# Gram stages whose first transfers go out between TensorE's first chunks, a 3x3 convolution that begins slot by slot, and smaller first loads, in a two-layer bottleneck kernel

## The chip, the core and the metric

The kernel runs on one core of a Trainium2 chip. The time is device microseconds of one execution, from three executions of the same program. A profile of one more execution gives the times of the single instructions. TensorE multiplies matrices, VectorE (DVE), ScalarE (ACT) and GpSimd (POOL) work on elements, and SyncE (SP), ScalarE and GpSimd issue DMA transfers. Everything is float32.

## What is computed

Two bottleneck layers follow one another on a batch of 64 images with 1024 channels of 14 x 14 pixels. Each layer is a 1x1 convolution to 256 channels, a 3x3 convolution and a 1x1 convolution back to 1024, each followed by a batch normalization over the whole batch, with a residual at the end:

```python
def _bn(x, gamma, beta):
    mean = jnp.mean(x, axis=(0, 2, 3), keepdims=True)
    var = jnp.var(x, axis=(0, 2, 3), keepdims=True)
    xn = (x - mean) * jax.lax.rsqrt(var + EPS)
    return gamma.reshape(1, -1, 1, 1) * xn + beta.reshape(1, -1, 1, 1)
out = jax.nn.relu(_bn(_conv(x, w1, b1, 1, 0), g1, be1))
out = jax.nn.relu(_bn(_conv(out, w2, b2, 1, 1), g2, be2))
out = _bn(_conv(out, w3, b3, 1, 0), g3, be3)
out = jax.nn.softplus(residual_scale)[0] * out
out = x + out
return jax.nn.relu(out)
```

A batch normalization needs the statistics of all pixels before the first pixel can go on. That cuts each layer into stages, and at each cut TensorE waits until the statistics are there.

## The kernel before

The 256 middle channels lie as two **slots** of 128 partitions each in one resident tile `y` of 128 x 2 x 12544 elements (12544 pixels, the whole batch). The stages, with their place in the profile in microseconds:

- **First 1x1 convolution** (0 to 308). `plain_conv1` does images 0 and 1 of the pixel tiles, with weights `w` that `load_w1` brings in four transfers on ScalarE's queue and pixel tiles `x` that `load_x` brings on SyncE's queue (the first tile in four transfers). All later tiles go through `Conv1`, a product scheme with seven multiplications in place of eight (class `Seven`), whose weight sums `ws` `combine_w1` makes on VectorE. Beside it the 3x3 filters of both layers are transformed (`filters`) and written to memory as `u`.
- **3x3 convolution** (308 to 599), `conv2`. It works on groups of 8 images (eight groups), each as six products over rows (L657 `Products`), in three pairs. For the first group `first_norm` normalizes the pixels (ScalarE the rows from 7 on, VectorE rows 0 to 6), slot 1 first; `combine` makes the row combinations `t`, `r`, the half sums `sums`, the differences `diffs` and `v`, and fetches the filters `ua` and `ub` for each product. TensorE multiplies into `even`, `odd`, `m` and `l`, and `finish` puts the results together on VectorE. The scales and shifts of the normalization come from `affine_by_slot` (L1119), which calls `affine` once for each slot before `conv2` begins.
- **Gram stage** (600 to 687), `gram`. The statistics of the third convolution are not taken from its results. They follow from the sum and the Gram matrix (256 x 256) of the normalized pixels, which needs all pixels transposed. The stage goes in 49 **chunks** of 256 pixels. For the first six (`FIRST`) and the last one (`LAST`) TensorE transposes against an identity (`by_tensor`, L942, then a VectorE copy, L948, into one of six buffers `zt`). For the other 42 VectorE transposes blocks of 32 x 32 (`by_vector`, L954), from a copy in which blocks of 32 partitions have been laid out side by side. `spread(k)` makes that copy for six chunks by 16 transfers of 96 KB from `y` into one of two homes (`ws` and `home`): ten on SyncE's queue, six on GpSimd's. Before any of that, every piece of `y` is normalized on ScalarE (L538, in `bounds`) and has a constant subtracted on VectorE (`less`, L1248). Each chunk ends in four Gram products on TensorE (`cp`, `ap`).
- **End of the statistics, third convolution and residual** (687 to 1300 for layer 0, with the first convolution of layer 1 woven in; 1677 to 2002 for layer 1).

Layer 1 repeats the 3x3 convolution from 1300 and the Gram stage from 1592.

What sets the order of work around the change: each engine runs its instructions in the order in which they stand. A planner may move an instruction ahead of its place in the program, unless it was recorded with `keep_in_program_order`; TensorE's instructions and the VectorE transposes (L954) have that, the `less` pieces, the copies into `zt` and the small operations of `affine` do not. All `norm` and `less` pieces stand in the program ahead of the first `spread`, and both `spread(0)` and `spread(1)` stand ahead of the first chunk:

```python
bounds = [0, CH * P, 3 * CH * P, *range(GPX, NPX + 1, GPX)]
for a, e in zip(bounds, bounds[1:]):
    for s in range(MS):
        y = y_all[:, s, a:e]
        norm(s, y, aff)
        less(s, y)
...
ready = [spread(k) for k in range(2)]
```

With `start = FIRST * CH * P`, the first `spread` covers pixels 1536 to 3071, for which the pieces up to pixel 3136 must be ready.

Of the kernel before, what the change touches and what calls it, by code (L numbers as in the profile page):

```python
# [41 lines left out]
P = 128  # L42
# [14 lines left out]
FIRST, LAST = 6, 1  # L57
# [36 lines left out]
def bottlenecks(ctx: ExitStack, tc: tile.TileContext, x, w1s, w2s, w3s, pars, out):  # L94
# [40 lines left out]
    def load_w1(pool, b, queue):  # L135

        w = pool.tile([P, MS, 2, CS // 2, P], FP, tag="w1", name=f"w1_{b}")
        for h in range(2):
            for o in range(MS):
                queue.dma_start(out=w[:, o, h], in_=w1s[b][:, o, h])  # L140
        return w
# [398 lines left out]
    def norm_vector(s, y, aff):  # L540
        scale, shift = aff
        nc.vector.tensor_scalar(y, y, scale[:, s : s + 1], shift[:, s : s + 1], ALU.mult, ALU.add)
        nc.vector.tensor_scalar(y, y, 0.0, None, ALU.max)

    def conv2(psum, pool, b, par, aff, stats):
# [29 lines left out]
        def stt(to, a, by, c):  # L575
            nc.vector.scalar_tensor_tensor(to, a, by, c, ALU.mult, ALU.add)  # L576

        def combine(g, pair, before=None):
# [4 lines left out]
            def ready(i, r):  # L583
                lines = (full if i in (3, 4) else RT) * GI
                r = r.rearrange("p s r (i w) -> p s (r i) w", i=GI)

                def half(tag):
                    return pool.tile([P, MS, RT * GI, WH], FP, tag=tag, name=tag, bufs=BUFS[tag])[:, :, :lines]

                sums, diffs = half("sums"), None  # L590
                nc.vector.tensor_add(sums, r[:, :, :, WH:], r[:, :, :, :WH])  # L591
                if i in FOUR:
                    diffs = half("diffs")
                    nc.gpsimd.tensor_sub(diffs, r[:, :, :, :WH], r[:, :, :, WH:])  # L594
                    v = pool.tile([P, MS * RT * GI * W], FP, tag="v", name="v", bufs=BUFS["v"])
                    v = v[:, : MS * lines * W].rearrange("p (s l c) -> p s l c", s=MS, c=W)
                    q = r.rearrange("p s l (q c) -> p (s l) q c", q=2)
                    nc.vector.tensor_sub(
                        v[:, :, :, 1 : W - 1].rearrange("p s l (q c) -> p (s l) q c", q=2),
                        q[:, :, :, 1:], q[:, :, :, : WH - 1],  # L600
                    )
                    nc.scalar.activation(v[:, :, :, 0], r[:, :, :, 0], AF.Copy)
                    nc.scalar.activation(v[:, :, :, W - 1], r[:, :, :, W - 1], AF.Copy, scale=-1.0)
                    r = v

                u = []
                for tag, a, e in (("ua", 0, 1), ("ub", 1, NKS[i])):
                    n = MS * MS * (NK - 1 if a else 1) * P
                    v = pool.tile([P, n], FP, tag=tag, name=tag, bufs=BUFS[tag])
                    v = v[:, : MS * MS * (e - a) * P].rearrange("p (s o k m) -> p s o k m", s=MS, o=MS, m=P)  # L610
                    nc.sync.dma_start(
                        out=v.rearrange("p s o k m -> p (s o) (k m)"),
                        in_=us[b][i][:, :, :, a:e].rearrange("p s o k m -> p (s o) (k m)"),
                    )
                    u.append(v)
                return Products(i, lines, r, sums, diffs, u, first=g == 0 and i == order[0][0])

            both = slice(0, MS)
            if pair[0] == 1:
                t1, t2 = new("t"), new("t")  # L620
                slots = [both] if before is None else [slice(s, s + 1) for s in reversed(range(MS))]
                for part in slots:
                    if before is not None:
                        before(part.start)
                    last(t1, g, 2, -3.0, part)
                    last(t2, g, 1, -3.0, part)
                    for s in range(part.start, part.stop):
                        stt(t1[:, s, :full], rows(g, s, 2, 0, full), -4.0, rows(g, s, 4, 0, full))
                        stt(t2[:, s, :full], rows(g, s, 1, 0, full), -4.0, rows(g, s, 3, 0, full))
                    nc.vector.tensor_add(ra[:, part], t1[:, part], t2[:, part])  # L630
# [227 lines left out]
        def first_norm(s):  # L858

            top = 7  # L860
            norm(s, y_grp[:, s, 0, top:], aff)
            norm_vector(s, y_grp[:, s, 0, :top], aff)
# [47 lines left out]
    def gram(psum, pool, homes, aff, less, beside):  # L910
# [7 lines left out]
        zts = itertools.cycle(zts)  # L918
        start = FIRST * CH * P

        bounds = [0, CH * P, 3 * CH * P, *range(GPX, NPX + 1, GPX)]
        for a, e in zip(bounds, bounds[1:]):
            for s in range(MS):
                y = y_all[:, s, a:e]
                norm(s, y, aff)
                less(s, y)

        def spread(k):

            x = homes[k % 2][:, : MS * STEP].rearrange("p (s j f) -> p s j f", s=MS, j=4)  # L930
            for i, j in itertools.product(range(4), range(4)):
                queue = nc.gpsimd if (4 * i + j) % 8 in (2, 5, 7) else nc.sync
                a = start + k * STEP + i * RUN
                queue.dma_start(out=x[32 * i : 32 * i + 32, :, j], in_=y_all[32 * j : 32 * j + 32, :, a : a + RUN])
            return x.rearrange("p s j f -> p (s j) f")

        def by_tensor(a):
# [10 lines left out]
            nc.vector.tensor_copy(zt[:, :, :M], tp.rearrange("p (c m) -> p c m", c=CH))  # L948
# [12 lines left out]
        def pairs():  # L961
            for i in range(FIRST):
                yield by_tensor(i * CH * P)
            for k in range(STEPS):
                x = ready.pop(0)
                for i in range(RUN // (CH * 32)):
                    yield by_vector(x, i)
                if k + 2 < STEPS:
                    ready.append(spread(k + 2))
            for i in range(LAST):  # L970
                yield by_tensor(NPX - (LAST - i) * CH * P)

        ready = [spread(k) for k in range(2)]
# [138 lines left out]
    def aggregate(stats, first):  # L1112
        n = stats.shape[1]
        mv = small.tile([P, n, nc.vector.BN_AGGR_DIM], FP, tag=f"mv{n}", name="mv")
        for o in range(n):
            nc.vector.bn_aggr(mv[:, o, :], stats[:, o, first:, :].rearrange("p t f -> p (t f)"))
        return mv

    def affine_by_slot(stats, first, par, g, be, order):  # L1119

        both = [small.tile([P, MS], FP, tag=f"by_slot_{n}", name=n) for n in ("scale", "shift")]
        for s in order:
            mv = aggregate(stats[:, s : s + 1], first)
            affine(mv, 1, par, g + s, be + s, to=[v[:, s : s + 1] for v in both])
        return both

    def affine(mv, n, par, g, be, conv_bias=None, to=None):

# [3 lines left out]
        v, sd, r, q = tl("v"), tl("sd"), tl("r"), tl("q")  # L1134
        nc.scalar.activation(sd, mv[:, :, 1], AF.Sqrt, bias=eps)
        nc.vector.tensor_scalar(v, mv[:, :, 1], EPS, None, ALU.add)
        nc.vector.reciprocal(r, sd)

        scale, shift = to or (tl("scale"), tl("shift"))
        nc.vector.tensor_mul(q, r, v)  # L1140
        nc.vector.scalar_tensor_tensor(q, q, -0.5, r, ALU.mult, ALU.mult)
        nc.vector.tensor_mul(r, r, par[:, g : g + n])
        nc.vector.scalar_tensor_tensor(scale, q, 1.5, r, ALU.add, ALU.mult)
        if conv_bias is None:
            off = mv[:, :, 0]
        else:
# [3 lines left out]
            nc.vector.tensor_add(off, mv[:, :, 0], bias)  # L1150
            nc.vector.tensor_sub(off, off, bias)
        nc.vector.scalar_tensor_tensor(shift, off, -1.0, scale, ALU.mult, ALU.mult)
        nc.vector.tensor_add(shift, shift, par[:, be : be + n])
        return scale, shift

    def softplus(par):
# [6 lines left out]
        u, w, l, d, z = tl("u"), tl("w"), tl("l"), tl("d"), tl("z")  # L1163
# [24 lines left out]
    with tc.tile_pool(name="first", bufs=1) as one, tc.tile_pool(  # L1188
# [4 lines left out]
        pair = [load_x(xpool, 0, t, 4 if t == 0 else 2) for t in range(2)]  # L1193
        for b in range(2):
            p = keep.tile([P, NPAR], FP, tag=f"par{b}", name=f"par{b}")
            nc.scalar.dma_start(out=p, in_=pars[b][:, :NPAR])
            par.append(p)
        masks.make_identity(nc, ident)
# [24 lines left out]
    for b in range(2):  # L1223
        pb = par[b]
        sp = softplus(pb)
        minus_c = keep.tile([P, MS], FP, tag="minus_c", name="minus_c")
        nc.vector.tensor_scalar(minus_c, pb[:, BE2 : BE2 + MS], 0.0, -1.0, ALU.max, ALU.mult)

        aff = affine_by_slot(stats1, T - 3 + b, pb, G1, BE1, (1, 0))
        stats2 = keep.tile([P, MS, 1 + len(LAST_PARTS), nc.vector.BN_STATS_DIM], FP, tag="stats2", name=f"stats2_{b}")  # L1230
        with tc.tile_pool(name=f"conv2_{b}", bufs=1) as pool, ExitStack() as scope:
            conv2(Psum(scope, ["l"], l=2, m=2, odd=2, even=2), pool, b, pb, aff, stats2)

        with tc.tile_pool(name=f"last_{b}", bufs=1) as one, tc.tile_pool(
# [5 lines left out]
            aff = affine(aggregate(stats2, 0), MS, pb, G2, BE2)  # L1240
            with ExitStack() as scope:
# [4 lines left out]
                with tc.tile_pool(name=f"gram_{b}", bufs=1) as pool:  # L1246
                    def less(k, y):
                        nc.vector.tensor_scalar(y, y, minus_c[:, k : k + 1], None, ALU.add)  # L1248

# [15 lines left out]
                    grams = gram(psum, pool, homes, aff, less, beside)  # L1265
# [6 lines left out]
                aff = affine(mv3, CS, pb, G3, BE3, conv_bias=B3)  # L1272
                for a in aff:
                    nc.vector.tensor_scalar(a, a, sp, None, ALU.mult)
# [48 lines left out]
```

## Time and profile before

| what | before |
| --- | --- |
| median of three executions | 2007.07 us (2005.67 to 2010.76) |
| the profiled execution | 2004.56 us, span 2002.8 us |
| TensorE (PE) busy | 1945.9 us, 97% of the span |
| VectorE (DVE) busy | 1586.3 us, 79% |
| ScalarE (ACT) busy | 948.3 us, 47% |
| GpSimd (POOL) busy | 618.5 us, 31% |
| chain that ended last | PE 79%, DVE 13%, DMA 4% |
| first convolution, TensorE's first matmul | at 5.89 us |
| 3x3 convolution, first matmul on data | at 315.85 us (layer 0), 1308.10 us (layer 1) |
| Gram stage, first transpose on TensorE | at 604.59 us (layer 0), 1595.90 us (layer 1) |
| memory traffic | 267.95 MB read, 115.87 MB written |

The span is the time between the first and the last instruction of the profiled execution; its device time is 1.8 us longer. "Busy" is the time in which an engine worked on an instruction. The chain that ended last goes back from the last instruction, at each step to what released it. TensorE is busy for all but 57 us of the span, so what can be won without less arithmetic lies in those microseconds, and in stretches in which TensorE's granted clock is low: the profile gives that clock as a share of full speed for each stretch.

### The profile page before, as it was taken

The numbers are of one execution on the slowest core, as the hardware profiler recorded it, in microseconds if no ns is written. First come the engines' busy times: TensorE is split into PE (matmuls) and PEld (weight loads), VectorE is DVE, ScalarE is ACT, GpSimd is POOL, SyncE is SP. The second block draws the span as 40 slices with busy tenths as digits, with TensorE's granted clock in tenths as the row PEclk, the third lists the DMA queues.
The fourth block names the chain that finished last, engine by engine and source line by source line (L and its number), as shares of the span: only waits on it lengthen the run. The fifth ranks groups of instructions, "written<-read, shape, count | busy, mean of one in ns | idle before, by whom it ended". The sixth has DMA issues, their size and how long they took to land.

```text
span 2002.8 us, 27581 instructions
## 1 busy us (share of the span) xinstructions
PE 1945.9 (97%) x9560; PEld 1640.7 (82%) x9560; DVE 1586.3 (79%) x2842; ACT 948.3 (47%) x1933; POOL 618.5 (31%) x690
## 2 busy tenths in 40 slices
PE   8999998999997999999999999999999889999999
PEld 4555557999996889999999999989999877555554
DVE  5788758999986567776776777699999865899997
ACT  1322214366655055555555555444656631555555
POOL 0111101122214123334333333212121140666665
PEclk9999999999997999999999999999999999999999
DMA  7866724555546624444444444265656375699998
GB/s 270 285 251 248 256 97 164 179 190 197 181 142 177 215 105 185 162 185 170 167 188 161 176 179 163 96 204 176 199 178 199 117 183 199 252 335 331 340 339 298
DMA packets 176219, 407.65 MB, mean 204 GB/s; under 512 B 12368, under 2 KB 143504, under 8 KB 159568
## 3 DMA queue, kind: packets, MB, share of 16 engines
q1 hardware_dynamic: 162208, 330.44, 48.4%
q10 hardware_dynamic: 5328, 50.86, 6.1%
q0 software_dynamic: 8544, 24.59, 3.7%
q8 instruction: 76, 1.25, 0.2%
q14 instruction: 63, 0.52, 0.1%
HBM read 267.95 MB, written 115.87 MB: 192 GB/s over the span
## 4 chain that ended last, share of the span: by engine, by line
PE 79%; DVE 13%; DMA 4%; ACT 1%; issue 1%; POOL 1%; SPq 1%; DVEq 0%; ACTq 0%
PE ay L171 16%; PE cy L171 13%; PE cp L171 11%; PE ap L171 10%; PE odd L171 5%; PE even L171 5%; PE ax L171 5%; PE m L171 5%; PE l L171 4%; PE cx L171 4%; DMA x<-mid 2%; DVE x L455 2%; DVE sums L591 1%; PE ps L171 1%; DMA out<-x 1%
## 5 line engine op out<-in xcount | busy, mean ns | idle before, releaser
L329 ACT ACTIVATE cu<-cy,scale 128x196 f32<-128x196 f32 (+1 forms) x552 | 257.4, 475 | 295.9 <-PE cy L171 288.3
L329 ACT ACTIVATE x<-x,shift 128x392 f32<-128x392 f32 x368 | 211.8, 614 | 68.8 <-POOL x L481 52.9
L455 DVE SCALAR_TENSOR_TENSOR x<-cp,scale,x 128x196 f32<-128x196 f32 (+1 forms) x368 | 178.0, 484 | 82.5 <-PE cp L171 81.1
L594 POOL TENSOR_TENSOR diffs<-r 128x448 f32<-128x448 f32 (+1 forms) x80 | 111.5, 1405 | 424.5 <-DVE r L576 263.4
L171 PE MATMUL cy<-ct,ws 128*128 128x196 f32 (+1 forms) x736 | 222.0, 383 | 2.5 <-ACT cu L329 2.5
L476 POOL TENSOR_TENSOR x<-x,cu 128x196 f32<-128x196 f32 (+1 forms) x184 | 167.4, 910 | 170.8 <-ACT cu L329 170.7
L171 PE MATMUL ay<-at,ws 128*128 128x196 f32 (+1 forms) x752 | 209.4, 382 | 1.0 <-ACT au L329 1.0
L481 POOL TENSOR_TENSOR x<-x,cu 128x392 f32<-128x392 f32 x124 | 125.8, 1014 | 191.1 <-DVE x L455 186.4
L171 PEld LDWEIGHTS ay<-at,ws 128*128 128x128 f32 x752 | 136.4, 190 | 35.0 <-ACT au L329 2.0
L171 PEld LDWEIGHTS cy<-ct,ws 128*128 128x128 f32 x736 | 133.7, 190 | 36.9 <-ACT cu L329 3.8
L502 POOL TENSOR_TENSOR x<-x,cu 128x392 f32<-128x392 f32 x120 | 125.0, 1042 | 82.7 <-DVE x L455 77.6
L171 PE MATMUL m<-sums,ua 128*128 128x224 f32 (+1 forms) x752 | 145.5, 336 | 0.0
L171 PE MATMUL cp<-zt 128*128 128x257 f32 x392 | 123.0, 396 | 16.2 <-DVE zt L954 16.2
L171 PEld LDWEIGHTS m<-sums,ua 128*128 128x128 f32 x752 | 131.4, 190 | 0.2
L455 DVE SCALAR_TENSOR_TENSOR x<-cx,scale,x 128x196 f32<-128x196 f32 (+1 forms) x184 | 89.2, 485 | 50.5 <-PE cx L171 50.1
L171 PE MATMUL cy<-y,w 128*128 128x196 f32 (+1 forms) x404 | 126.0, 398 | 0.0
L171 PE MATMUL cx<-y,w 128*128 128x196 f32 (+1 forms) x404 | 125.2, 396 | 0.0
L171 PE MATMUL even<-v,ub 128*128 128x224 f32 (+1 forms) x640 | 123.8, 335 | 0.7 <-ACT even L688 0.7
L171 PE MATMUL odd<-v,ub 128*128 128x224 f32 (+1 forms) x640 | 123.9, 335 | 0.2
L171 PE MATMUL l<-diffs,ub 128*128 128x224 f32 (+1 forms) x640 | 122.0, 334 | 0.0
L329 ACT ACTIVATE au<-ay 128x196 f32<-128x196 f32 (+1 forms) x141 | 53.8, 381 | 139.7 <-PE ay L171 139.0
L171 PE MATMUL cp<-y,ws 128*128 128x196 f32 (+1 forms) x368 | 113.9, 391 | 2.5 <-DVE x L455 1.0
(215 smaller groups left out, 4355.9 us busy)
## 6 DMA issues: line engine op xcount, KB each, us to landing
x<-in_x SPq DMA_DIRECT2D x62, 1568.0 KB, 6.8
ub<-u SPq DMA_DIRECT2D x80, 768.0 KB, 4.8
x<-mid SPq DMA_DIRECT2D x32, 1568.0 KB, 10.1
mid<-x ACTq DMA_DIRECT2D x31, 1568.0 KB, 5.2
out<-x SPq DMA_DIRECT2D x124, 392.0 KB, 6.7
ua<-u SPq DMA_DIRECT2D x96, 256.0 KB, 3.1
ub<-u SPq DMA_DIRECT2D x16, 1024.0 KB, 6.2
u<-y POOLq DMA_DIRECT2D x40, 256.0 KB, 6.3
```

The costliest lines, as they stand in the source:

```text
L171: tc.keep_in_program_order(nc.tensor.matmul(*args, **kw))
L329: tc.keep_in_program_order(nc.scalar.activation(*args, **kw))
L455: nc.vector.scalar_tensor_tensor(v, bank, self.scale[:, o : o + 1], v, ALU.mult, ALU.add)
L476: nc.gpsimd.tensor_add(self.part(1, 1), self.part(1, 1), u3)
L481: nc.gpsimd.tensor_add(v, v, self.u12)
L502: nc.gpsimd.tensor_add(v, v, self.u12[:, i * self.n : (i + 1) * self.n])
L591: nc.vector.tensor_add(sums, r[:, :, :, WH:], r[:, :, :, :WH])
L594: nc.gpsimd.tensor_sub(diffs, r[:, :, :, :WH], r[:, :, :, WH:])
```

## The change

Five edits, in the order of the kernel's stages.

**Smaller first loads.** The first of the four weight transfers is cut in two, and the first pixel tile comes in eight transfers in place of four. The softplus of both layers' residual scale is computed at the start of the program, where before each layer asked for its own at the start of its second stage.

```diff
+        n = CS // 2
+        for h, o in itertools.product(range(2), range(MS)):
+
+            step = n // 2 if b == h == o == 0 else n
+            for s in range(0, n, step):
+                queue.dma_start(out=w[:, o, h, s : s + step], in_=w1s[b][:, o, h, s : s + step])
...
-        pair = [load_x(xpool, 0, t, 4 if t == 0 else 2) for t in range(2)]
+        pair = [load_x(xpool, 0, t, CS if t == 0 else 2) for t in range(2)]
...
+        sps = [softplus(p) for p in par]
```

**The 3x3 convolution begins slot by slot.** `affine_by_slot` is gone. `first_norm(s)` now computes the scale and shift of its own slot first, so the order on VectorE is: statistics, scale and normalization of slot 1, its `t` and `r`, and then the same for slot 0. VectorE takes rows 0 to 5 in place of 0 to 6. These VectorE operations are recorded in program order. The filters of the very first product come as four transfers: `ub` for slot 1, `ub` for slot 0, then `ua` for each; before, they were `ua` and then `ub`, one transfer each.

```diff
         def first_norm(s):
 
-            top = 7
+            affine_of(s)
+            top = 6
             norm(s, y_grp[:, s, 0, top:], aff)
             norm_vector(s, y_grp[:, s, 0, :top], aff)
...
+                first = g == 0 and i == order[0][0]
+                u = {}
+                for tag, a, e in (("ub", 1, NKS[i]), ("ua", 0, 1)) if first else (("ua", 0, 1), ("ub", 1, NKS[i])):
...
+                    for part in [slice(1, 2), slice(0, 1)] if first else [slice(0, MS)]:
+                        nc.sync.dma_start(
+                            out=v[:, part].rearrange("p s o k m -> p (s o) (k m)"),
+                            in_=us[b][i][:, part, :, a:e].rearrange("p s o k m -> p (s o) (k m)"),
+                        )
```

**The small operations of `affine`** stand in program order; the negated mean is made early, and for up to two slots the shift is one operation per slot in place of two operations in a row:

```diff
+        run(nc.vector.tensor_scalar(minus, off, -1.0, None, ALU.mult))
+        run(nc.vector.reciprocal(r, sd))
...
+                    nc.vector.scalar_tensor_tensor(
+                        shift[:, one], scale[:, one], minus[:, one], par[:, be + s : be + s + 1], ALU.mult, ALU.add
+                    )
```

**Gram stage.** Seven chunks come from TensorE's transposes at the start and none at the end. The first `spread` covers pixels 768 to 2303, right behind the first three chunks, and is issued after chunk 1; the second is issued after chunk 5. The pieces of `norm` and `less` are made as they are needed (`norm_to`), between the chunks, in other sizes and with slot 1 first; VectorE does both steps for slot 1 of the first piece. The `less` pieces and the copies into `zt` are recorded in program order, so they cannot pass the transposes. Of the 16 transfers, nine go to SyncE's queue and seven to GpSimd's.

```diff
-FIRST, LAST = 6, 1
+FIRST, LAST = 7, 0
...
+        head = 3 * CH * P
         start = FIRST * CH * P
+        bounds = [0, CH * P, head, head + STEP, *range(2 * GPX, NPX + 1, GPX)]
+        pieces = list(zip(bounds, bounds[1:]))
+
+        def less(s, y):
+            tc.keep_in_program_order(nc.vector.tensor_scalar(y, y, minus_c[:, s : s + 1], None, ALU.add))
+
+        def norm_to(end):
+
+            while pieces and pieces[0][0] < end:
+                a, e = pieces.pop(0)
+                for s in reversed(range(MS)):
+                    y = y_all[:, s, a:e]
+                    if a == 0 and s == 1:
+                        norm_vector(s, y, aff, minus_c[:, s : s + 1])
+                    else:
+                        norm(s, y, aff)
+                        less(s, y)
 
         def spread(k):
 
+            first = start + k * STEP if k else head
+            norm_to(first + STEP)
...
-                queue = nc.gpsimd if (4 * i + j) % 8 in (2, 5, 7) else nc.sync
+                queue = nc.gpsimd if 4 * i + j in (1, 3, 6, 8, 10, 13, 15) else nc.sync
...
         def pairs():
+
+            norm_to(head)
+            then = {
+                1: lambda: ready.append(spread(0)),
+                2: partial(norm_to, 2 * GPX),
+                4: partial(norm_to, 3 * GPX),
+                5: lambda: ready.append(spread(1)),
+            }
             for i in range(FIRST):
-                yield by_tensor(i * CH * P)
+                a = i * CH * P
+                yield by_tensor(a if a < head else a + STEP)
+                if i in then:
+                    then[i]()
...
-        ready = [spread(k) for k in range(2)]
+        ready = []
```

The weight sums for the next stage (`combined`) are made at the same count of chunks from the front plus one, which is now after the last chunk.

## The prediction

> **What bounds the kernel now.** I read TensorE's own waits first, since TensorE is busy for 1945.9 of 2002.8 us. Each line gives the waiting engine, what it waited for, total us, times and the longest:
>
> ```profile
> PE cp L171 <- DVE zt L954: 16.2, 2, 8.1
> PE cy L942 <- DVE y L1248: 10.7, 2, 5.4
> PE even L171 <- DVE t L576: 7.6, 2, 3.8
> PE ps L171 <- DMA w<-in_w: 5.9, 1, 5.9
> ```
>
> These four are 40.4 of TensorE's 57 idle us, and each occurs once per layer, the last once in all. The change touches each of them: line 1 is the wait for the first VectorE transposes of the Gram stage, line 2 the entry into that stage, line 3 the entry into the 3x3 convolution, line 4 the start.
>
> Next the timeline of layer 0's Gram stage (start, duration), which tells why line 1 is there:
>
> ```profile
> 614.04 8.07 SPq L934 DMA_DIRECT2D ws<-y  x10
> 619.69 5.19 POOL L934 DMA_DIRECT2D home<-y  x6
> 622.23 6.56 SPq L934 DMA_DIRECT2D home<-y  x10
> 626.85 1.31 DVE L954 STREAM_TRANSPOSE zt<-ws 128x512 f32<-128x512 f32 x2 [0.49 <-DMA home<-y]
> 627.62 1.23 PE L171 MATMUL cp<-zt 128*128 128x257 f32 x2 [8.08 <-DVE zt L954]
> ```
>
> The first spread starts to issue at 614.04, needs 8.07 us of SyncE's queue, and its last bytes land just before 626.85. TensorE has finished its six own chunks at 619.54 and stands still for 8.08 us. The view by stretches of time (length, busy PE, PE loads, DVE, ACT, POOL, granted clock, DMA share, GB/s) tells what the gap costs besides:
>
> ```profile
> 616.00:620.00 4.00, 3.54 (x24) 3.09 (x22) 4.00 (x6) 4.00 (x3) 4.00 (x6) 1.00 0.86 226
> 620.00:624.00 4.00, 0.00 (x0) 0.00 (x0) 2.87 (x4) 4.00 (x4) 4.00 (x6) 0.75 0.98 214
> 624.00:628.00 4.00, 0.38 (x1) 0.38 (x2) 2.96 (x4) 4.00 (x3) 0.88 (x1) 0.50 0.84 252
> 628.00:632.00 4.00, 4.00 (x13) 3.41 (x13) 4.00 (x6) 2.05 (x2) 0.00 (x0) 0.50 0.32 76
> 632.00:636.00 4.00, 4.00 (x25) 3.63 (x24) 3.77 (x8) 0.00 (x0) 2.34 (x5) 0.97 0.29 74
> ```
>
> After the gap the clock is at half until about 631.85: 13 matmuls in four us, then 25.
>
> Last, the same view of the 3x3 convolution shortly after its entry:
>
> ```profile
> 340.00:350.00 10.00, 10.00 (x60) 9.96 (x59) 10.00 (x17) 5.00 (x13) 1.43 (x1) 1.00 0.70 230
> 350.00:360.00 10.00, 10.00 (x55) 9.91 (x54) 10.00 (x21) 2.15 (x5) 0.00 (x0) 1.00 0.59 186
> 360.00:370.00 10.00, 10.00 (x59) 9.92 (x58) 10.00 (x22) 3.53 (x11) 2.05 (x3) 1.00 0.45 144
> ```
>
> VectorE (third busy column) is full too. The chain of waits runs through VectorE from 342 to 408, but for 2.4 us of ScalarE at 372, and only then returns to TensorE. So here TensorE and VectorE arrive together, and a head start for TensorE alone gains nothing.
>
> **The Gram stage, step by step** (layer 0; layer 1 shows the same waits, 8.1 and 5.3 us). Durations: `less` on 512 elements 0.49, on 1568 1.03 (so 1536 about 1.0, 832 about 0.6); copy into `zt` 0.69; VectorE transpose 0.66; a chunk's Gram products 1.32 warm, 2.57 at half clock (607.76 to 610.34); its TensorE transposes 0.65 warm, 1.31 cold. ScalarE's normalization takes 0.3, 0.55, 1.5 and 1.57 us for 256, 512, 1536 and 1568 elements.
>
> Entry. The dependent operations before the first normalization are 0.2 us apart; two shift operations in a row become one, so scale and shift are ready at 603.1 in place of 603.42. VectorE does slot 1 of the first piece itself (two operations, about 0.35 each). ScalarE's part still takes 0.63 us from issue to VectorE's start, as before. TensorE begins at about 604.3, 0.3 earlier; nearly all of line 2 stays.
>
> I follow VectorE's new order. After the pieces to pixel 768 (605.3) come the copies of chunk 0 (606.5) and chunk 1 (607.7), then the two pieces of 1536 (ScalarE has them by 607.7), done at 609.7: **the first spread issues at 609.7 in place of 614.04**. Nine issues on SyncE at about 0.65 (8.07 us over ten before, with two slow ones) plus 2.3 us to the last landing (spread 4 issues 648.35 to 655.02, its transposes start at 657.35) give 618 to 620. TensorE meanwhile works seven chunks: cold to about 611, chunk 1 done at 612.2, then 2 us a chunk, chunk 5 at 620.2. VectorE's copy of chunk 6 stands behind two `less` pieces of 1568 (618.4 to 620.4), so chunk 6 runs 621.2 to 622.5, after a wait of 1.0. What is queued behind that copy are the VectorE transposes; the first is done by 621.8, in time. So **chunk 7 starts at 622.5**, where before chunk 6 started at 627.62.
>
> From there 42 chunks at 1.32 end at 677.9; before, the last product ended at 686.92. That is **9.0 us**. It has three parts: the gap of 8.08 less the new wait of 1.0 and what the extra chunk takes, and the half-speed stretch of 4.23 us, worth 2.1. Here the Trainium skill (TensorE: Matmul & The Clock Gate, "What's actually happening") says that the clock drops after one idle window of some 3.4 us and needs as long busy to return. That would make the stretch worth 1.7, not the 2.1 of the row; I take the row. The rule also says that the wait of 1.0 leaves the clock alone, and the idle 0.81 us before 308.85, followed by a clock of 1.00, agrees.
>
> Later spreads. Spread 1 waits for `less` to 620.4, so at 8.2 to 9 us from issue to landing (648.35 to 657.35 is 9.0 with ten issues) it lands at 628.6 to 629.4; TensorE needs the first of its chunks at 630.4, VectorE 0.7 earlier. Spreads 2 to 5 each have two `less` pieces (2.0 us) ahead of them that before were long done. In the trace SyncE issues those spreads back to back (640.41 to 640.51, 648.26 to 648.35), 7 to 7.75 us each against TensorE's 7.9 per spread; with nine issues it gains 0.7, and the pieces fit beside SyncE's earlier issues. Cost: nothing to 1.5, taken as 0.8. The weight sums after the last chunk (eight of 0.69 in layer 0, 5.5 us) stand ahead of the copy of the Gram matrix, but VectorE leads TensorE by up to six buffers, 7.9 us, so they are covered. **Net 8.2 per layer, 5 to 10.**
>
> **The 3x3 entry.** TensorE's first matmul on data at 315.85 is put down to VectorE's `t` (315.82), but `ub` is also only there at 315.7: issued at 309.51, 1024 KB, 6.2 us to landing in the list of transfers. Halved and first in line (308.76), slot 1's 512 KB should land near 313.2. [...] Slot 1's `r` is ready at 313.0 (313.59 before). So TensorE starts some 2.7 us earlier, with an idle time of 1.1 in place of 3.74, which also keeps the clock: the pass that took 315.85 to 321.5 at half speed takes 3 us less.
>
> Against it: VectorE's two slots were interleaved, each dependent small operation hiding beside the other slot's; in a row, slot 0's `r` is done at 317.35 in place of 316.54, 0.8 later, even with 0.3 saved by rows 0 to 5. Everything after is VectorE's full queue to 408. In layer 0 VectorE has about 1 us of idle time up to 340 (0.8 waiting for `m`) that an earlier TensorE gives back; in layer 1 there is 0.2. So **zero in layer 0, 0.5 lost in layer 1**; bounds: 3 gained to 1.5 lost each.
>
> **The start.** The first matmul waits for the first 256 KB of `w`, landed at 5.84. In the stretches of 2 us, 196 and 306 GB/s flow from 2 us on. With 128 KB of `w` and 196 KB of `x` as the first need, about 324 KB against 650 KB must have moved: some 1.3 us earlier. No more than eight transfers of these two queues are in flight in the built program, so the later pieces wait for earlier ones; they are needed only from about 12 us on. Softplus now stands ahead of the weight sums on VectorE; `ws` is needed at 32.98, and the sums were done at 12.5, so 17 us of cover remain. **1.3 gained, 0 to 2.** TensorE's row of products to 308 passes it on.
>
> **Sum.** 1.3 + 2 x 8.2 - 0.5 + 0.4 (0.2 per layer in the last `affine`, one dependent operation fewer) = 17.6 us. On the profiled execution's 2004.56 that is 1987.0; the median lies 2.5 above it, so **1989.5**.
>
> **Rivals.**
> - *Everything arrives (B).* If VectorE is not the bound up to 408, the 3x3 entry's 2.7 us and the clock's 3 us come through, some 5 per layer: 1979. For it: TensorE is as full as VectorE. Against: that chain. 12%.
> - *Half of the gap stays (C).* The first spread lands as slowly as before (12.8 us from first issue): 609.7 + 12.8 = 622.5, 1.4 late; spread 1, at 620.4 + 12.8, comes 3.4 late, and a drop of the clock costs 2 more. 8.2 becomes 3: 2000. For it: DMA is at 0.98 while both spreads are in flight. Against: spread 1 now goes out 10 us later, so they do not overlap. 18%.
> - *Slower (D).* Pinned on VectorE, `less` delays every spread: each waits for six transposes, then 2.0 us of `less`, then its issue and landing of 9. If SyncE's backlog hides none of it, spreads 1 to 6 are each 3.5 us late at TensorE, 21 us a layer against 9 gained: 2 x 12 - 1.3 lost, 2030. It decides from 1.5 us per spread on. For it: VectorE's transposes start 2.8 us after they could (657.35), so landing times are near the need. Against: TensorE does not wait once after 631. 8%.
>
> The forecast (A) has 62%. A and B, and nearly all of C, are faster. About 0.3% (6 us) is what a measurement of this kernel tells from no change: faster 0.87, within 0.3% 0.05, slower 0.08. The range of 1979 to 2001 takes in A's bounds (5 to 10 per layer, entry and start), B's edge and most of C.
>
> **What would show it.** Right: the wait for `zt` at the first VectorE transposes falls from 8.1 to 1 or 2, the clock stays at 1.00 from 612 of the stage on, the first matmul comes at 4.5, the 3x3 products begin at about 1.5 us after the zeroing matmuls but TensorE waits 3 us in all before group 3. Wrong: new waits for `zt` at every sixth chunk, or a 3x3 stage shorter by 3 us or more.

## The result, and the profile after

| | before | after |
| --- | --- | --- |
| median | 2008.84 us (2005.67 to 2010.76, four executions) | 1996.01 us (1994.34 to 1996.83, four) |
| ratio | | 0.9937, 95% interval 0.9919 to 0.9954 |
| profiled execution, its span | 2004.56, 2002.8 us | 1996.83, 1995.0 us |
| VectorE busy, GpSimd busy | 1586.3, 618.5 us | 1592.6, 634.5 us |

The kernel became 12.8 us faster. Sign and range of the prediction hold, its sum of 17.6 us does not. The landmarks of the two traces show where the time went. A 3x3 stage is counted from its first zeroing product to its last product, a Gram stage from there to the last Gram product, the statistics to the end of the products with `ones`, and the final stage from there to TensorE's end.

| stage | before | after | shift predicted | shift measured |
| --- | --- | --- | --- | --- |
| to the 3x3 convolution of layer 0 | 308.85 | 307.07 | -1.3 | -1.8 |
| 3x3, layer 0 | 290.4 | 292.7 | 0 | +2.3 |
| Gram, layer 0 | 87.8 | 77.2 | -8.2 | -10.7 |
| statistics, layer 0 | 13.4 | 14.9 | 0 | +1.5 |
| fused stage between the layers | 600.6 | 600.5 | 0 | -0.1 |
| 3x3, layer 1 | 289.5 | 292.9 | +0.5 | +3.4 |
| Gram, layer 1 | 86.8 | 77.6 | -8.2 | -9.2 |
| statistics, layer 1 | 13.0 | 14.5 | 0 | +1.4 |
| final stage | 307.7 | 312.3 | 0 | +4.6 |

So the Gram stages gave 19.9 us, more than forecast, and five stages that were to stay about as they were gave 13 back. TensorE's waits in the profile after (waiting instruction, what it waited for, total us, times, longest) show both sides:

```profile
PE cy L969 <- DVE y L939: 11.0, 3, 5.2
PE even L174 <- ACT even L698: 6.8, 4, 2.9
PE ps L174 <- DMA w<-in_w: 4.8, 1, 4.8
...
PE even L174 <- DVE r L642: 3.5, 3, 1.3
...
PE even L174 <- ACT even L700: 2.6, 4, 0.9
PE cp L174 <- DVE zt L975: 1.7, 2, 0.9
```

The 16.2 us for `zt` are down to 1.7. The wait for the first loads is 1.1 shorter, and the entry into the Gram stage (first line) stays at 5.2 per layer, as forecast. New are the second and fifth lines: 9.4 us for `even`, inside the 3x3 convolution.

The timeline of layer 0's Gram stage after (start, duration):

```profile
609.99 6.81 SPq L961 DMA_DIRECT2D ws<-y  x9
617.11 7.01 SPq L961 DMA_DIRECT2D home<-y  x9
619.48 0.68 DVE L975 COPY zt<-ay 128x512 f32<-128x512 f32 x1
620.08 3.67 DVE L981 STREAM_TRANSPOSE zt<-ws 128x512 f32<-128x512 f32 x6
620.22 0.70 PE L174 MATMUL cp<-zt 128*128 128x257 f32 x2 [0.85 <-DVE zt L975]
```

The first spread goes out at 609.99 (forecast 609.7), and VectorE's first six transposes run in one go from 620.08, without a wait for a transfer. Behind the entry, TensorE's longest stop is 0.85 us, at the seventh chunk. By stretches of time (length, busy PE, PE loads, DVE, ACT, POOL, granted clock, DMA share, GB/s):

```profile
616.00:620.00 4.00, 3.38 (x22) 2.89 (x20) 4.00 (x6) 4.00 (x3) 2.63 (x3) 1.00 0.77 210
620.00:624.00 4.00, 3.78 (x22) 3.48 (x23) 4.00 (x8) 4.00 (x4) 2.30 (x5) 1.00 0.89 227
624.00:628.00 4.00, 4.00 (x26) 3.64 (x26) 2.68 (x4) 4.00 (x3) 3.95 (x7) 1.00 0.96 227
628.00:632.00 4.00, 4.00 (x26) 3.67 (x25) 4.00 (x7) 1.78 (x2) 1.44 (x3) 1.00 1.02 248
```

Before, the same rows fell from 24 matmuls to none, and to a clock of 0.50. Now every row holds 22 to 26 matmuls at full clock. The 3x3 convolution, in the same view:

```profile
340.00:350.00 10.00, 10.00 (x54) 9.91 (x54) 9.87 (x16) 2.35 (x6) 1.18 (x1) 1.00 0.72 234
350.00:360.00 10.00, 7.27 (x32) 6.73 (x31) 10.00 (x20) 1.83 (x5) 0.00 (x0) 0.83 0.24 84
360.00:370.00 10.00, 10.00 (x61) 9.93 (x60) 10.00 (x21) 3.21 (x10) 2.42 (x2) 1.00 0.43 136
```

In the middle row TensorE stands still for 2.73 us in front of the second group's first product and loses a part of its clock (32 matmuls where there were 55). VectorE is full in the same ten microseconds. That row is what the experiments set out from.

### The profile page after: what moved, and what is told of

Read it like the earlier page. It is cut to its first block, busy times and chain, and to the rows that moved or that the text cites. A ratio compares the mean times of both kernels' runs of the same rounds, so it can differ in the third digit from the quotient of the medians.

```text
span 1995.0 us, 27618 instructions
## 1 busy us (share of the span) xinstructions
PE 1944.6 (97%) x9560; PEld 1640.3 (82%) x9560; DVE 1592.6 (80%) x2848; ACT 945.1 (47%) x1931; POOL 634.5 (32%) x704
## 4 chain that ended last, share of the span: by engine, by line
PE 79%; DVE 14%; DMA 3%; issue 1%; ACT 1%; POOL 1%; DVEq 0%; SPq 0%; ACTq 0%; POOLq 0%
PE ay L174 17%; PE cy L174 13%; PE cp L174 11%; PE ap L174 10%; PE odd L174 5%; PE even L174 5%; PE ax L174 5%; PE m L174 4%; PE cx L174 4%; PE l L174 4%; DMA x<-mid 2%; DVE x L458 2%; DVE r L582 1%; DMA out<-x 1%; DVE f L753 1%
## 5 line engine op out<-in xcount | busy, mean ns | idle before, releaser
L600 POOL TENSOR_TENSOR diffs<-r 128x448 f32<-128x448 f32 (+1 forms) x80 | 120.2, 1516 | 414.4 <-DVE r L582 262.8
```

## The experiments

After the result, two theories stood. Theory 1 said: the Gram stage brings the whole gain, and the new entry into the 3x3 convolution costs 2 to 3.5 us a layer because VectorE decides there and comes later. Theory 2 said: the entry is neutral, and the losses are scatter.

**Undoing the entry, and each half of it.** The first kernel takes back the entry's edits, the second only the transfers, the third only VectorE's slot order, and the fourth is the changed kernel again.

```diff
-            affine_of(s)
-            top = 6
+            top = 7
...
-                for tag, a, e in (("ub", 1, NKS[i]), ("ua", 0, 1)) if first else (("ua", 0, 1), ("ub", 1, NKS[i])):
+                for tag, a, e in (("ua", 0, 1), ("ub", 1, NKS[i])):
...
-                    for part in [slice(1, 2), slice(0, 1)] if first else [slice(0, MS)]:
+                    for part in [slice(0, MS)]:
```

> The changed kernel with the entry of the 3x3 convolution put back as it was (both slots' scale and shift interleaved and unpinned, rows 0 to 6 on VectorE, ua and ub each one transfer in the old order, the first group's operations unpinned); start, Gram stage and last affine stay changed. Theory 1: the new entry costs 2.3 us in layer 0 and 3.4 in layer 1, because VectorE is the bound up to group 3 and gets there later; so this kernel is 5 to 6 us faster than the changed one (about 1990.5), and the stretch from the first zeroing matmul to the last 3x3 product shrinks by 2 to 3.5 us per layer. Theory 2: the new entry is neutral and the losses of the profile are phases of the clock and scatter; then the time stays within 2 us of the changed kernel's 1996.0. Theory 3 (the new entry gains, something else loses): 3 to 5 us slower than the changed kernel, about 2000.

> The changed kernel with only the loads of ua and ub put back (ua first, each in one transfer). VectorE's slots stay in a row. Theory 1: TensorE's first 3x3 products fall back from 2.6 to about 5 us behind the zeroing start plus a colder clock, but VectorE decides until group 3; the time stays within 2 us of the changed kernel's. If instead the halves are what gains here, 3 us per layer are lost, about 2002. If the early start itself is what costs (by moving VectorE's planned order), this kernel gains 3 to 5 us.

> The changed kernel with VectorE's entry put back (slots interleaved and unpinned, rows 0 to 6), while ub still comes first and in halves. Theory 1: slot 0 is ready 0.8 us earlier and VectorE's queue with it; gains 1 to 3 us per layer over the changed kernel, 1990 to 1994. Theory 2: within 2 us of 1996.

> The changed kernel once more, for a second profile. Theory 1: the stretches of both 3x3 convolutions are again 2 to 3.5 us longer than before's 290.4 and 289.5 (first zeroing matmul to last product); the final stage, 300.6 us in the first profile of the changed kernel against 296.2 before, comes out between these, because that difference is scatter of a stage full of transfers. Rival: the final stage is again 4 us longer; then it is an effect of the change.

| kernel | median us | ratio to before (interval) | 3x3 stage, layers 0 and 1 |
| --- | --- | --- | --- |
| before | 2005.80 | | 290.4, 289.5 |
| changed, again | 1995.71 | 0.9947 (0.9932 to 0.9962) | 292.7, 292.9 |
| old entry | 1989.65 | 0.9917 (0.9900 to 0.9935) | 289.8, 289.6 |
| `ub` whole | 1989.26 | 0.9916 (0.9900 to 0.9932) | 290.7, 291.1 |
| old slot order | 1991.99 | 0.9929 (0.9915 to 0.9944) | 291.4, 291.6 |

The second profile of the changed kernel repeats its 3x3 stages to 0.1 us: Theory 2 falls. With the old entry the kernel is 6.1 us faster than with the new one. The slots in a row cost 0.9 and 1.5 us of the two stages (`ub` whole against old entry), and 1.3 and 1.3 where the halves are in (changed against old slot order). The 0.9 is at the edge of scatter, since the old entry's layer 0 took 289.5 to 290.4 us in four profiles, and in the medians `ub` whole and the old entry are level. The halves cost 2.0 and 1.9. That is a miss: taking the halves back was to leave the time within 2 us, and it gained 6.4, more even than the 3 to 5 of that expectation's last branch. Of the 6.4, 3.9 lie in the two 3x3 stages; by the profiles, a final stage of 308.7 us in place of 311.2 is the largest other piece. Before's final stage took 307.7.

The medians of before differ between the sets of runs (2005.80 us here, 2008.13 and 2009.16 below), so each ratio is to the before of its own set.

**Each part alone on the kernel before.** All three kernels also carry the last `affine`'s new order and the early softplus.

> The kernel before with the Gram stage's edits alone (seven own chunks, first transfers from between the chunks, less pinned, nine to seven issues), beside the last affine's new order and softplus ahead of the loop; first loads and the 3x3 entry are before's. Theory 1: the Gram stage brings nearly the whole gain, 9.5 to 10.5 us a layer from the last 3x3 product to the last Gram product (77.2 to 78 us in place of 87.8 and 86.8), less 1 to 1.5 a layer that the statistics behind it lose by the clock: 14 to 18 us below before's 2005.8, 1988 to 1992, as fast as or faster than the whole change. Theory 2 (all parts gain a little): 2000 or above.

> The kernel before with the new 3x3 entry alone (slots in a row, ub first and in halves, pins), beside the last affine's new order and softplus ahead of the loop. Theory 1: TensorE gets ahead of VectorE, stands still for about 2.7 us at the first product of the second group, and its clock drops there; together with VectorE's lateness at 390 to 410 that costs 2 to 3.5 us a layer: 4 to 7 us slower than before, 2010 to 2013. Theory 2 (the loss belongs to the combination with the Gram stage): within 2 us of before's 2005.8.

> The kernel before with the smaller first loads, beside the last affine's new order and softplus ahead of the loop. The first matmul comes at 4.3 to 4.8 in place of 5.9; 1 to 1.5 us less in all: 2004 to 2005. A rival holds that the start is lost in the scatter of TensorE's row of products to 308, then 2005 to 2007.

| kernel | median us | ratio to before's 2008.13 (interval) | difference |
| --- | --- | --- | --- |
| Gram stage alone | 1989.08 | 0.9907 (0.9889 to 0.9925) | -18.7 us |
| entry alone | 2016.40 | 1.0042 (1.0028 to 1.0056) | +8.4 us |
| first loads alone | 2007.94 | 1.0000 (0.9990 to 1.0011) | 0 |

The sum, -10.3, agrees with the -12.8 of the whole within the intervals. The entry alone costs more than expected; 5.6 of it lie in the two 3x3 stages (292.8 and 292.8 us), and its profile shows 3.0 more in the two statistics, which the entry does not touch. The first loads do bring the first matmul forward, from 5.89 to 4.34, and at the end of layer 0's Gram stage that profile is still 3.8 us ahead. In the two statistics it loses 5.3.

**Is it the early start or the order of other engines?** The planner that lays out the operations answered the new transfers with another order. On VectorE, pieces of `f`, `r` and `sums` change places from 326 us on; on ScalarE, pieces of `v` come 2 to 5 us later. So the halves change TensorE's start and the order of both these engines. With the halves sent in the other order, VectorE and ScalarE keep the changed order and TensorE loses its start:

```diff
-                    for part in [slice(1, 2), slice(0, 1)] if first else [slice(0, MS)]:
+                    for part in [slice(0, 1), slice(1, 2)] if first else [slice(0, MS)]:
```

> The changed kernel with the two halves of ub in the other order: slot 0's half, which TensorE needs second, goes out first. VectorE's planned order is that of the changed kernel, operation by operation, but TensorE's first 3x3 products start about as late as with the whole transfer, at 313 to 313.5. Theory 1a (TensorE's early start is what costs: it runs ahead of VectorE, stands still 2.7 us at the second group's first product and loses its clock there): the stop is 2.1 us or less, the clock stays at 1.00, and this kernel is 3 to 6 us faster than the changed one, 1990 to 1993. Theory 1b (the planner's other order of VectorE's operations costs): the time stays at 1995 to 1997.

It took 1994.88 us (0.9934, 0.9917 to 0.9950), with 3x3 stages of 292.8 and 292.9. TensorE's data products began 5.2 us after the zeroing ones, less late than expected, where it was 4.2 in the changed kernel and 6.8 with the whole transfer. In layer 0 the stop at the second group shrank to 1.7 us, and the clock stayed at 1.00:

```profile
350.00:360.00 10.00, 8.28 (x46) 7.85 (x45) 10.00 (x20) 2.86 (x7) 0.00 (x0) 1.00 0.36 118
```

In layer 1 a stop of 1.8 us was left and the clock still fell (0.85 from 1340 to 1350 us). Nothing was gained in either. Layer 1 has the opposite case too. The kernel of the last experiment below has the 3x3 convolution of the changed kernel, and behind the same stop (2.86 us in the changed kernel, 2.88 there) one lost its clock and the other kept it. First the changed kernel, then that one:

```profile
1340.00:1350.00 10.00, 10.00 (x48) 9.79 (x48) 10.00 (x21) 2.69 (x9) 2.42 (x2) 0.84 0.12 36
```

```profile
1340.00:1350.00 10.00, 10.00 (x55) 9.93 (x56) 10.00 (x21) 3.54 (x11) 1.73 (x2) 1.00 0.31 98
```

Both stages took 292.9 us. So the stop and the clock that it costs are not the cause. What is left is the order of VectorE and of ScalarE, and the transfers themselves (`ua` now comes last). No run divides these; what follows looks at VectorE, which is full.

**What is dear in that order.** In the changed kernel's timeline, GpSimd's `diffs` and VectorE's operations beside them:

```profile
330.68 4.12 POOL L600 TENSOR_TENSOR diffs<-r 128x448 f32<-128x448 f32 x2 [5.95 <-DVE r L582]
...
333.68 2.06 DVE L782 TENSOR_TENSOR fa<-f 128x896 f32<-128x896 f32 x1
335.67 1.08 DVE L783 TENSOR_TENSOR fb<-f 128x896 f32<-128x896 f32 x1
...
361.90 2.42 POOL L600 TENSOR_TENSOR diffs<-r 128x336 f32<-128x336 f32 x2 [17.29 <-DVE r L582]
362.58 0.88 DVE L848 TENSOR_SCALAR center<-mv_first 128x2 f32<-128x2 f32 x1
```

`fa` and `fb` are the same work, 1.08 us each. But `fa` begins at 333.68 while `diffs` runs until 334.80, and takes 2.06. `center` has two elements per partition and takes 0.88 us beside `diffs`. The same operations with `ub` whole:

```profile
332.45 1.60 POOL L600 TENSOR_TENSOR diffs<-r 128x448 f32<-128x448 f32 x1 [1.49 <-DVE r L582]
...
334.78 1.08 DVE L782 TENSOR_TENSOR fa<-f 128x896 f32<-128x896 f32 x1
```

There `diffs` has ended at 334.05, and `fa` takes its 1.08. From 307 to 427 us GpSimd's 16 `diffs` take 24.8 us in the changed kernel and 20.5 with `ub` whole, and VectorE's side adds up: `fa` 1.0, six `y` 1.0, `center` and a `stats` 1.5 and twelve `r` 0.7 longer with 0.8 us of waiting, less 2.8 that `sums` saves, gives 2.2 us for the 2.0 that the stage lost. The Trainium skill (SBUF — State Buffer, "Who interferes with whom") has the rule for it: the two engines share one pair of ports, a VectorE operation with two inputs in SBUF contends with a GpSimd operation that reads SBUF, and not with one that only writes; the later one stands still. `fa` is such an operation, and the trace agrees: it begins while `diffs` has 1.12 us to run, and takes 0.98 us longer than its usual 1.08. For one with a single input, like `center`, the page names modes that take both ports. So the test is to let GpSimd write only. In two kernels it fills `diffs` with zeros:

```diff
-                    nc.gpsimd.tensor_sub(diffs, r[:, :, :, :WH], r[:, :, :, WH:])
+                    nc.gpsimd.memset(diffs, 0.0)
```

> The changed kernel, in which GpSimd writes zeros into diffs and reads nothing, so the differences of the column halves are left out of the convolution. VectorE's and TensorE's orders are those of the changed kernel, operation by operation. Theory 1c (VectorE's other order costs because other of its operations fall on GpSimd's diffs and both stretch): VectorE's stretched operations shrink to their usual length (fa from 2.06 to 1.08 us, center and stats from 0.9 to 0.15), and the 3x3 stage of layer 0 falls from 292.7 us to within 0.7 of what its twin with the whole transfer takes. Rival 1d (the order itself is worse, whatever GpSimd does): it stays about 2 us longer than the twin.

> The twin: the kernel with ua and ub whole, as in the earlier run, in which GpSimd writes zeros into diffs. Its orders are those of that earlier kernel. With the differences read it took 290.7 us for layer 0's 3x3 stage and 291.1 for layer 1's. Theory 1c: 289 to 290.7, and the other twin within 0.7 of it. Rival 1d: the other twin about 2 us longer in each layer.

| GpSimd's part | halves first: median, 3x3 stages | `ub` whole: median, 3x3 stages |
| --- | --- | --- |
| reads `r` | 1995.71 us; 292.7, 292.9 | 1989.26 us; 290.7, 291.1 |
| writes zeros | 1978.24 us; 284.9, 285.1 | 1982.30 us; 285.6, 288.2 |

To before's 2009.16 us in this set the two kernels with zeros have ratios of 0.9850 (0.9823 to 0.9877) and 0.9872 (0.9843 to 0.9901). Rival 1d falls: the order that cost 2 us with GpSimd's reads costs nothing without them. Theory 1c expected too little: the twin's 285.6 us lie under its 289 to 290.7, and both kernels lose 3 to 8 us of their 3x3 stages. The kernel with the halves is now the shorter one, by 0.6 and 3.1 us, the second outside the 0.7 that was expected; these two runs do not tell its start from its order. VectorE's rows, and a row of stretches, of the kernel with the halves and zeros:

```profile
L782 DVE TENSOR_TENSOR fa<-f 128x896 f32<-128x896 f32 x1 | 1.1, 1086 | 0.0
...
L848 DVE TENSOR_SCALAR center<-mv_first 128x2 f32<-128x2 f32 x1 | 0.2, 159 | 0.0
```

```profile
350.00:360.00 10.00, 10.00 (x56) 9.93 (x55) 10.00 (x24) 3.01 (x9) 0.47 (x1) 1.00 0.39 130
```

The operations have their usual lengths (mean ns after the bar), VectorE gets through 24 operations in these ten microseconds in place of 20, and TensorE's stop is gone. What this pair leaves open is how much is due to the ports alone: a fill also no longer waits for `r`, nor holds `r` back, and it is short (7.4 us of GpSimd from 307 to 427 in place of 24.8).

**The pins of the Gram stage.**

```diff
-            tc.keep_in_program_order(nc.vector.tensor_scalar(y, y, minus_c[:, s : s + 1], None, ALU.add))
+            nc.vector.tensor_scalar(y, y, minus_c[:, s : s + 1], None, ALU.add)
...
-            tc.keep_in_program_order(nc.vector.tensor_copy(zt[:, :, :M], tp.rearrange("p (c m) -> p c m", c=CH)))
+            nc.vector.tensor_copy(zt[:, :, :M], tp.rearrange("p (c m) -> p c m", c=CH))
```

> The changed kernel with the Gram stage's less and the copies into zt left to the planner; it then puts several less pieces ahead of the copies of TensorE's last own chunks and all of them ahead of the second spread's transposes. Theory 1: the first spread's gain stays, but TensorE waits 2 to 4 us more for the copies of chunks 5 and 6 (behind three to five pieces of 1.0 us), which may drop its clock: 2 to 5 us a layer back, 2000 to 2006. Rival: VectorE leads by enough, and the time stays within 2 us of 1996.

It took 2000.29 us (0.9961, 0.9945 to 0.9976), with Gram stages of 81.0 and 80.9 us: some 3 to 4 a layer back, as expected in size. The place differs. Its timeline:

```profile
619.45 1.97 DVE L939 TENSOR_SCALAR y<-y,minus_c 128x1568 f32<-128x1568 f32 x2
621.96 1.04 DVE L939 TENSOR_SCALAR y<-y,minus_c 128x1568 f32<-128x1568 f32 x1 [0.54 <-ACT y L541]
623.07 3.68 DVE L981 STREAM_TRANSPOSE zt<-ws 128x512 f32<-128x512 f32 x6
623.84 1.23 PE L174 MATMUL cp<-zt 128*128 128x257 f32 x2 [2.67 <-DVE zt L981]
```

The own chunks' copies are in time. The first VectorE transposes are queued behind three `less` pieces that nobody needs yet, one of them waiting for ScalarE. TensorE stands still for 2.67 us, and its next products take twice as long (1.23 us for two, 0.60 after that). This is not the prediction's rival D, in which pinned pieces delay the transfers: here unpinned pieces delay the transposes, once per layer, and the pins are what keeps them back.

**The final stage.** Here half of the stores of the paired tiles are left out:

```diff
-                    out=self.to[i].rearrange("p (s f) -> p s f", s=CS)[:, q::step, :], in_=self.xt[i][:, q::step, :]
+                    out=self.to[i].rearrange("p (s f) -> p s f", s=CS)[:, q : q + 1, :], in_=self.xt[i][:, q : q + 1, :]
```

> The changed kernel, in which the last stage stores only one of each two channel groups of its pairs (half of these stores are left out of the output). Every engine's order is that of the changed kernel. If the last stage gives back 4 us because transfers now bound it, TensorE's time from the last ones-product of layer 1 to its end falls from 311 to 312 us to 304 to 306, and its waits for DVE x from 3.7 us to under 1. If that stage's length is scatter of another kind, it stays at 309 to 312.

The changed kernel's waits in the last stage, and its transfers from 1720 to 1970 us:

```profile
POOL x L505 <- DMA x<-mid: 3.9, 3, 1.3
PE cp L174 <- DVE x L458: 3.7, 4, 2.1
```

```profile
DMA packets 31060, 82.22 MB, mean 329 GB/s; under 512 B 2016, under 2 KB 27716, under 8 KB 27716
```

With half the stores the mean is 251 GB/s, both waits are gone (GpSimd waits 4.9 us for stores instead), and the stage takes 308.1 us in place of 312.3 and 311.2; the time is 1993.14 (0.9921, 0.9894 to 0.9948). The expected 304 to 306 was not reached, and late loads are not shown to be the cause. With the first loads alone, all stores in, GpSimd waits longer for its loads than in the changed kernel:

```profile
POOL x L505 <- DMA x<-mid: 5.3, 4, 1.3
```

That stage took 307.6 us. What goes with the stage's length is TensorE's wait for VectorE's `x`. Over all fourteen profiles, stages with 0 to 0.9 us of it took 307.6 to 308.1 us, those with 1.4 to 1.8 took 308.7 to 309.3, and those with 2.8 to 3.8 took 310.6 to 312.3. What brings this wait about stays open. It came with the new Gram stage (307.8 to 312.3 us with all stores in, 307.6 to 308.1 in the three profiles with the old one), and it varies.

## Why the prediction was right, and where it failed

**The Gram stage: mechanism right, size low.** The first spread went out at 609.99 (forecast 609.7), the seventh chunk waited 0.85 (1.0), the eighth began at 621.64 (622.5), and the clock was at 1.00 from 612 on. From 621.64 to 676.98 the 42 chunks took 1.32 each without one wait. The part brought 10.7 and 9.2 us in place of 8.2, and two terms were mis-sized. The 0.8 us set aside for later spreads was not needed; the second spread went out at 617.11, where 620.4 was forecast. And in layer 0 TensorE's own chunks were to run cold to about 611, but the clock was back at 609.32. TensorE worked 4.3 us at half clock there, where the forecast had 6.7; by estimate the difference is worth 1.2 us. That is luck in part: before had 7.2 us at half clock at this place in layer 0 and 5.8 in layer 1, after it was 4.3 and 5.3. Alone the part is worth 18.7 us (15.1 to 22.3) in the median, where 16.4 was forecast.

**The 3x3 entry: the failed step.** "Everything after is VectorE's full queue to 408" fits, and so does the step that a head start of TensorE alone would not come through: it began 4.6 us earlier and waited. What failed is "zero in layer 0, 0.5 lost in layer 1". That sum carried over VectorE's operations of before, with their lengths and in their order, and gave the 0.8 us by which slot 0 comes later to idle time. The runs show three things in its place. With the slots in a row the stage is 0.9 to 1.5 us longer, which fits the 0.8 coming through to its end; no trace follows it there. The planner lays VectorE's next 70 us out anew when the transfers change. And the lengths are not a property of the operation: beside `diffs` the same `fa` takes 2.06 for 1.08. This gave 2.3 and 3.4 us where at most 1.5 each had been allowed. Sending first the half that TensorE needs first did what the prediction wanted of it (products 4.2 us after the zeroing ones, 6.8 with the whole), and the kernel was 6.4 us slower with the halves.

**The rivals.** B ("everything arrives") needed VectorE not to be the bound. It did not happen. The kernel with zeros in `diffs` takes 1978.24 us, close to B's 1979, but by chance: VectorE is full there too. C (half the gap stays) and D (each spread late) did not happen; no wait for `zt` came at a sixth chunk.

**The start.** The first matmul came at 4.82 and in repeats at 4.2 to 4.7 (forecast 4.5). In the median of the edit alone nothing of it is left, with an interval of 2 us to both sides, so 1.3 us can be neither shown nor excluded.

**What "untouched" stages did.** The prediction let the shift pass through the statistics and the final stage. In the statistics TensorE works on products of one column. Before:

```profile
698.53 1.93 PE L171 MATMUL ax<-ones,q 128*128 128x1 f32 x16
```

After:

```profile
688.35 3.55 PE L174 MATMUL ax<-ones,q 128*128 128x1 f32 x16
```

The same 16 products take 3.55 us because the clock was already down to 0.50, though TensorE was busy:

```profile
688.00:690.00 2.00, 2.00 (x11) 2.00 (x11) 0.00 (x0) 0.00 (x0) 0.00 (x0) 0.50 0.00 0
```

Over all the profiles these stages took 13.0 to 15.9 us, with no relation to the edits, and the profile of before lay at the short end in both layers. A part of what looked lost is thus a lucky profile, and the medians show 12.8 us where the profiles show 7.7. The 0.4 us of the last `affine` cannot be seen behind that.

The measured 1996.01 is therefore the forecast 1989.5 with a larger gain and three overlooked losses (entry, statistics, final stage). The first of these is traced to an edit; the other two are not. Three other kernels come out at the forecast figure: the Gram stage alone at 1989.08, with the new start and the old entry 1989.65, with the slots in a row but `ub` whole 1989.26. None of them confirms the sum, whose terms were off in both directions, but all three beat the change by 6 to 7 us.

## What to carry to other kernels

When a kernel's bound changes from stage to stage, credit an earlier start only as far as the next full engine, and ask what a planner makes of the edit: a transfer cut in two can reorder an engine that the edit does not name. Durations of VectorE operations beside GpSimd operations belong to the pair, so compare the busy time of both before an order is called equal. A pin is worth its line where an engine would otherwise fill its queue with work that nobody waits for yet.

## What the hardware showed unexpectedly

A small VectorE operation can cost as much as a large one: two elements per partition took 0.88 us beside `diffs`, 0.15 alone. Without GpSimd's reads of `r` the changed kernel's 3x3 stages are 7.8 us shorter in each layer.

How long TensorE stands still does not alone decide what its clock does. Behind the stop of 2.73 us in the changed kernel the granted clock was 0.50 for 3.41 us, and 16 products took 4.64 us that took 3.02 in the kernel with zeros. Stops of 3.00 us (old entry) and of 1.83 (halves swapped, layer 1) were followed by half clock as well. Stops of 2.08 (`ub` whole), 2.88 (half of the stores, layer 1) and 3.56 (`ub` whole, at the entry) were not.

In all fourteen traces, the stretches at half clock that end before the kernel does last 3.41, 6.83 or 10.24 us, multiples of 3.41. The Trainium skill (TensorE: Matmul & The Clock Gate, "What's actually happening") has a window of 3413 ns that runs freely, whatever the kernel does, and this agrees with it. The page also puts the low clock behind an idle window of about 3.4 us, and the prediction built on that. Here the measurement differs: no stop of 1.83 to 3.00 us holds such a window whole, and the clock fell. How much of a window must be idle these runs do not settle; a stop of 2 to 4 us may cost clock or not.
